# Two-layer graph attention on one core: a fourth query buffer in place of a product buffer, beta added a chunk later, and one pool of five PSUM banks

## The chip, the cores and the metric

The kernel runs on one core of one Trainium2 chip. The core has a matrix engine (TensorE: PE in the profile, with its weight loads as PEld), a vector engine (VectorE: DVE), a scalar engine (ScalarE: ACT), a general engine (GpSimd: POOL) and a synchronising engine (SyncE: SP). POOL issues the indirect DMAs (gathers and scatters) and SP issues most of the plain ones[...]. The metric is the device time of one execution in microseconds, as the median of several runs.

## The reference

The input x has 8 graphs of 2048 nodes with 256 features; one adjacency matrix of 2048 x 2048 holds for all of them, with about 0.4% of its entries set, the diagonal always.

Layer 0 is attention with 4 heads of 64. The scores are clipped to -10..10, masked entries are -10, and the softmax is taken in each chunk of 256 neighbours on its own:

```python
scores = jnp.clip(scores, -10.0, 10.0)
scores = jnp.where(mask == 0, jnp.asarray(-10.0, scores.dtype), scores)
attn = jax.nn.softmax(scores, axis=-1)           # over c within a chunk j
ctx = jnp.einsum('bhnjc,bhjcd->bhnd', attn, vc)
out = ctx @ Wo.T + bo + x                        # then a layer norm with gamma and beta
x = _layernorm(x + out)
```

Layer 1 is a graph attention: logits s_src + s_dst through a leaky ReLU, a softmax over the neighbours, the weighted sum of x @ W, an ELU, a residual and again a layer norm. Everything is float32.

## The kernel before

**Lists of neighbours.** At the start edge_lists (L45) turns each adjacency row into a list of at most 24 neighbours. Nodes are sorted by the number of their neighbours, so that a tile of 128 nodes shares one length (CAPS, L34: 24, 14, 13, 12, 11, 11, 10, 10, 9, 9, 8, 8, 7, 7, 6, 5). If a node has more neighbours than its tile allows, a dense path follows; with this input it does not run.

**Tables.** Two graphs are one group (G = 2; 4 groups). For a group, tables(g, t) (L344) makes for 128 nodes the keys and values (table kv_d in HBM, through the single buffer kvs) and the queries beside x + beta (table qx_d, through the single buffer qs and from xt). Every other call, chunk_x (L322) first transposes a chunk of 256 nodes on PE (L334). Chunks come in by load_x (L314) into two buffers xt; the same buffer takes beta in place on POOL (L352) and is written to qx_d by SP (L353). Only then may load_x fill it again.

**Attention of layer 0.** For each of 64 steps (group g, tile t), fetch0 (L504) gathers the neighbours' rows of kv_d, one indirect DMA (L469) for each place in the list, into "units" of two places, and then the tile's own row of qx_d into one of three buffers qx (L507). Units come from a ring of 14 (L39) that both layers share. scores0 (L511) multiplies keys by queries on DVE (L530); PE sums the products in parts of 8 columns by accumulating transposes (L541) into the bank pr, ACT copies this (L547), and a product with a 0/1 matrix (L551) leaves the scores in PSUM. A third of the units is instead multiplied in place and reduced by DVE alone (L555, L557). A product is laid over the keys of the unit before it; the first one has no such unit and goes into a buffer of its own, prod. softmax0 (L566) clips the scores (L571) and makes the weights; context0 (L588) weights the values (L481 on DVE, L487 on ACT) and PE sums them by accumulating transposes (L494). A step later finish0 (L607) makes the output and both norms; it reads x + beta from the second half of qx (L619, L625), which sets that buffer free. Another step later rows1 (L631) makes the rows of layer 1 (wh_d). In group 1 the lists for layer 1 are made from gathered rows on the way (ACT L459, DVE L460).

**Layer 1** works on two groups at once with the same tiles: fetch1, softmax1, context1, finish1 (L706).

**Order of the work.** The loop from L779 goes through 96 steps. Groups 0 and 1 are layer 0 alone, groups 2 and 3 alternate with the first half of layer 1, and the second half of layer 1 ends the program; while groups 0 to 2 run, the tables of the group after are made in the same steps. Within a group the tiles go from short lists (5) to the longest (24, the ninth step) and back to short ones (L740). In each step the gathers of the step after come first in the source:

```python
        if not tables_first:
            fetch(k + 1)
        scatters()
        if layer == 0:
            scores0(g, t)
            ...
            if g + 1 < NG:
                if i % 2 == 0 and i + NT + 2 < NG * NT:
                    load_x((i + NT + 2) // NT, (i + 2) % NT)
                tables(g + 1, i % NT)
```

The order within each engine's queue is not the source's: a planner lays the instructions of all engines out before the run, by priorities and its own estimate of durations, and adds the waits. The trace shows, for instance, table products of one step between the score transposes of the next. While the lists are made, first_tables (L403) makes the tables of group 0.

**PSUM** [...] Before, they are given out by name: acc two (the sums of both layers), tk two (all of the tables), tf two (scores, and the transposes of rows1), pr one, mf one (finish0, the products of rows1, finish1, and the preparation of the weights).

Of the kernel before, what the change touches and what calls it, by code (L numbers as in the profile page):

```python
# [44 lines left out]
def edge_lists(tc: tile.TileContext, pool, bank, adj, const, ident, rec_d, B, between):  # L45
# [118 lines left out]
    op = bank("mf", 1)[0:1, 0:1]  # L164
# [7 lines left out]
def sparse_path(ctx: ExitStack, tc: tile.TileContext, keep, x, adj, Wq, bq, Wk, bk, Wv, bv, Wo, bo, gamma, beta, W, a,  # L172
# [61 lines left out]
    with tc.tile_pool(name="prep", bufs=2) as prep:  # L234
        for dst, w, scale in ((wq, Wq, 0.125), (wkv[:, :, 0:F], Wk, 1.0), (wkv[:, :, F:], Wv, -1.0 / CH), (wo, Wo, 1.0)):
            wn = prep.tile([P, KC, F], F32, tag="wn", name="wn")
            nc.scalar.dma_start(wn, w.rearrange("(c p) f -> p c f", p=P))
            pt = bank("mf", 1).rearrange("p (c f) -> p c f", c=KC)
# [19 lines left out]
        pt = bank("mf", 1).rearrange("p (c f) -> p c f", c=KC)  # L258
# [4 lines left out]
        pa = bank("mf", 1)[:, 0:KC * 2 * H].rearrange("p (c e) -> p c e", c=KC)  # L263
# [24 lines left out]
        pt = bank("mf", 1)[:, 0:3 * KC].rearrange("p (k c) -> p k c", k=3)  # L288
# [33 lines left out]
    def chunk_x(g, t):  # L322
# [6 lines left out]
        for b in range(G):  # L329
            pt = bank("tk").rearrange("p (c r) -> p c r", r=CH)  # L330
# [12 lines left out]

    def tables(g, t):  # L344
        if t % 2 == 0:
            chunk_x(g, t)
        xT, xC, xt = xTs[g, t - t % 2]
        rows = slice(t % 2 * P, (t % 2 + 1) * P)
        if t % 2:

            xv = xt.rearrange("p k (b f) -> p (k b) f", b=G)
            nc.gpsimd.tensor_tensor(xv, xv, beta_r.unsqueeze(1).to_broadcast([P, 2 * G, F]), op=ALU.add)  # L352
            nc.sync.dma_start(qx_d[g][(t - 1) * P:(t + 1) * P, GF:].rearrange("(k p) f -> p k f", p=P), xt)  # L353
# [4 lines left out]
        for b in range(G):  # L358
            pm = bank("tk")
# [10 lines left out]
        q = bank("tk")  # L370
# [10 lines left out]
        if t == NT - 1:  # L381
# [4 lines left out]
            pv = bank("tk")[:, 0:KC * G].rearrange("p (c b) -> p c b", c=KC)  # L386
# [7 lines left out]
            po = bank("tk")[:, 0:KC * G].rearrange("p (c b) -> p c b", c=KC)  # L394
# [8 lines left out]
    def first_tables(t):  # L403
        if t == 0:
            load_x(0, 0)
        if t % 2 == 0 and t + 2 < NT:
            load_x(0, t + 2)
        tables(0, t)
# [95 lines left out]
    def fetch0(g, t):  # L504
        units = gather(kv_d[g].shape[1], kv_d[g], idx, t)
        qx = work.tile([P, 2 * GF], F32, tag="qx", name="qx", bufs=3)
# [4 lines left out]
    def scores0(g, t):  # L511
# [5 lines left out]
        npe = len(units) - len(units) // 3  # L517
        ps_sc = bank("tf")[:, 0:GH * S].rearrange("p (s e) -> p s e", e=GH)
# [3 lines left out]
        def product(i):  # L522

            u, s0, n = units[i]
            if i:
                room = units[i - 1][0][:, :, 0:GF]
            else:
                room = work.tile([P, UNIT, GF], F32, tag="prod", name="prod", bufs=1)
# [6 lines left out]
        for i in range(0, npe, 4):  # L535
            some = units[i:min(i + 4, npe)]
            pr = bank("pr", 1).rearrange("p (k r) -> p k r", r=P)
# [12 lines left out]
            for k, (u, s0, n) in enumerate(some):  # L550
                nc.tensor.matmul(ps_sc[:, s0:s0 + n, :], prT[0:n * W8, k, :], sel[0:n * W8, 0:n * GH],  # L551
                                 start=(s0 == 0), stop=(k == m - 1 and i + m == npe), skip_group_check=True)
# [226 lines left out]
    for k, (layer, i) in enumerate(seq):  # L779
# [6 lines left out]
        if layer == 0:  # L786
# [13 lines left out]
            if g + 1 < NG:  # L800
                if i % 2 == 0 and i + NT + 2 < NG * NT:
                    load_x((i + NT + 2) // NT, (i + 2) % NT)
# [452 lines left out]
```

## Time and profile before

| What | Value |
|---|---|
| median of 4 runs | 2458.81 us (2455.53 to 2466.82) |
| the profiled execution's own time | 2470.93 us |
| its span, first to last instruction | 2469.2 us |
| granted TensorE clock, mean | 0.882 |
| gathers from kv_d on POOL (L469) | 656, 1262 ns each |
| gathers from wh_d on POOL (L469) | 328, 1243 ns each |
| additions of beta on POOL (L352) | 32, 2478 ns each |
| bytes moved by DMA | 669.10 MB, mean 271 GB/s |
| DMA queue of the gathers, share of 16 engines | 58.4% |
| DMA queue of SP's transfers | 16.9% |

The profile is of one execution, whose own time is 0.5% above the median; shares and durations are read from it, and the medians are what is compared. A row of the groups gives line, engine, operation, the tiles written and read, how often, the busy time and the mean of one in ns, and behind the second bar the time that the engine stood idle just ahead of these instructions, with what ended it. A row of the waits gives who waited for whom: total, number of times, longest. Ends of matmuls are modelled, so a busy PE is not PE at its peak.

### The profile page before, as it was taken

Reading aid. Unit: us, or ns where it says so; the run is one execution under the profiler, and the core shown is the slowest. Engines: PE = TensorE matmul, PEld = TensorE weight load, DVE = VectorE, ACT = ScalarE, POOL = GpSimd, SP = SyncE. Lnnn points to the kernel's source line nnn. Section 1 sums busy time; section 2 is a strip of 40 time slices with the busy share of each in tenths; the row PEclk is TensorE's granted clock in tenths of the full one; section 3 lists DMA queues with packets and bytes.
Section 4 is the critical chain, followed back from the end, with each engine's and each line's share of the span. In section 5 each row is a group of like instructions: output and inputs, shape, how many; then the busy total and the mean of one; then the engine's idle time right before and its main releaser. Section 6 shows DMA issues by size and latency. Waiting matters only on the chain. (4 is left out here: it accounts for less than half of the span.)

```text
span 2469.2 us, 38911 instructions
## 1 busy us (share of the span) xinstructions
PE 1897.9 (77%) x11946; PEld 1622.9 (66%) x11946; DVE 1838.3 (74%) x4071; ACT 1404.6 (57%) x5011; POOL 1512.6 (61%) x1225
## 2 busy tenths in 40 slices
PE   6786787689888889889888988776867775455764
PEld 5675676578667778777777877665756665444653
DVE  5965567778656887767878899887878886556775
ACT  4572453355555556555546766765455677556766
POOL 1122755476544667556677886866768753757884
PEclk8998997799989899999999989887978897687887
DMA  6744977398967869888778998986679974986873
GB/s 227 271 161 156 347 266 257 132 325 300 320 237 263 285 198 355 292 301 302 258 255 298 363 344 281 340 291 244 227 243 343 353 282 172 376 288 228 281 269 109
DMA packets 240749, 669.10 MB, mean 271 GB/s; under 512 B 44455, under 2 KB 70826, under 8 KB 238486
## 3 DMA queue, kind: packets, MB, share of 16 engines
q0 software_dynamic: 156800, 505.01, 58.4%
q1 hardware_dynamic: 80016, 151.56, 16.9%
q10 hardware_dynamic: 3718, 9.97, 1.2%
q8 instruction: 98, 1.61, 0.3%
q14 instruction: 117, 0.96, 0.1%
HBM read 612.79 MB, written 126.36 MB: 299 GB/s over the span
## 5 line engine op out<-in xcount | busy, mean ns | idle before, releaser
L469 POOL DMA_INDIRECT u<-kv_d,idx x656 | 828.1, 1262 | 310.2 <-issue 127.8
L494 PE MATMUL acc<-ident,u 128*128 128x128 f32 x5248 | 729.3, 294 | 186.3 <-DVE u L481 107.3
L494 PEld LDWEIGHTS acc<-ident,u 128*128 128x128 f32 x5248 | 647.7, 153 | 255.7 <-DVE u L481 172.6
L469 POOL DMA_INDIRECT u<-wh_d,idx x328 | 407.6, 1243 | 152.4 <-issue 67.8
L481 DVE TENSOR_TENSOR u<-u,al 128x1024 f32<-128x1024 f32 x280 | 336.5, 1235 | 1.2
L481 DVE TENSOR_TENSOR u<-u,z 128x1024 f32<-128x1024 f32 x266 | 314.9, 1214 | 0.8
L487 ACT ACTIVATE u<-u,z 128x64 f32<-128x64 f32 x1008 | 259.2, 337 | 34.7 <-DVE z L678 34.7
L541 PE MATMUL pr<-ident,u 128*128 128x128 f32 x1472 | 209.4, 292 | 58.3 <-DVE u L530 54.3
L530 DVE TENSOR_TENSOR u<-u,qx 128x1024 f32<-128x1024 f32 x184 | 228.5, 1242 | 26.6 <-DMA u<-kv_d,idx 23.9
L541 PEld LDWEIGHTS pr<-ident,u 128*128 128x128 f32 x1472 | 179.4, 151 | 79.4 <-DVE u L530 71.7
L487 ACT ACTIVATE u<-u,al 128x64 f32<-128x64 f32 x800 | 206.8, 340 | 39.5 <-DVE al L585 36.7
L352 POOL TENSOR_TENSOR xt<-xt,beta_r 128x1024 f32<-128x1024 f32 x32 | 79.3, 2478 | 220.9 <-PE tk L334 179.6
L641 PE MATMUL mf<-wa,x1T 128*128 128x264 f32 x512 | 165.5, 450 | 33.8 <-ACT whs L644 17.6
L507 POOL DMA_INDIRECT qx<-qx_d,node x64 | 77.6, 1212 | 155.9 <-DVE o L625 94.1
L374 PE MATMUL tk<-wq,xT 128*128 128x256 f32 x512 | 146.0, 402 | 28.8 <-ACT kvs L368 28.8
L361 PE MATMUL tk<-wkv,xT 128*128 128x256 f32 x512 | 151.4, 411 | 15.7 <-ACT xC L339 15.5
L613 PE MATMUL mf<-wo,cT 128*128 128x256 f32 x512 | 141.8, 400 | 7.3 <-ACT whs L644 5.2
L641 PEld LDWEIGHTS mf<-wa,x1T 128*128 128x128 f32 x512 | 99.0, 215 | 71.8 <-ACT whs L644 34.0
L365 PE MATMUL tk<-wkv,xC 128*128 128x256 f32 x512 | 144.3, 397 | 0.0
L435 ACT ACTIVATE sq<-o,nm 128x256 bf16<-128x256 f32 x256 | 129.5, 506 | 5.0
L431 ACT ACTIVATE nm<-sums 128x2 f32<-128x2 f32 (+1 forms) x160 | 32.3, 202 | 168.2 <-DVE o L625 90.7
L374 PEld LDWEIGHTS tk<-wq,xT 128*128 128x128 f32 x512 | 93.7, 201 | 42.3 <-ACT kvs L368 33.0
(168 smaller groups left out, 3397.1 us busy)
## 6 DMA issues: line engine op xcount, KB each, us to landing
kv_d<-kvs SPq DMA_DIRECT2D x48, 512.0 KB, 6.3
wh_d<-whs SPq DMA_DIRECT2D x64, 260.0 KB, 5.2
xt<-in_x_dram SPq DMA_DIRECT2D x64, 256.0 KB, 4.7
qx_d<-xt SPq DMA_DIRECT2D x32, 512.0 KB, 3.8
qx_d<-qs SPq DMA_DIRECT2D x64, 256.0 KB, 6.1
x_d<-o SPq DMA_DIRECT2D x64, 256.0 KB, 5.3
xr<-x_d SPq DMA_DIRECT2D x32, 512.0 KB, 4.2
u<-kv_d,idx POOLq DMA_INDIRECT x656, 6.6
```

The costliest lines, as they stand in the source:

```text
L361: nc.tensor.matmul(pm[:, 0:F], xT[:, b * KC + kc, rows], wkv[:, kc, 0:F], start=(kc == 0), stop=False, skip_group_check=True)
L365: nc.tensor.matmul(pm[:, F:], xC[:, b * KC + kc, rows], wkv[:, kc, F:], start=False, stop=(kc == KC - 1), skip_group_check=True)
L374: nc.tensor.matmul(qb, xT[:, b * KC + kc, rows], wq[:, kc, :], start=(b == 0 and kc == 0), stop=False, skip_group_check=True)
L435: nc.scalar.activation(sq, src[:, k, :], AF.Square, bias=nm[:, k:k + 1], accum_out=m2[:, k:k + 1])
L469: nc.gpsimd.indirect_dma_start(out=u[:, k, 0:width], out_offset=None, in_=table, in_offset=bass.IndirectOffsetOnAxis(ap=idx[:, t, s0 + k:s ...
L481: nc.vector.tensor_tensor(pv, pv, av, op=ALU.mult)
L487: nc.scalar.activation(pe, pe, AF.Copy, scale=al[:, e, s0 + k:s0 + k + 1])
L494: nc.tensor.matmul(acc[:, c, :], part[:, k, c * P:(c + 1) * P], ident, is_transpose=True, start=first and k == 0 and c == 0, stop=last and ...
L530: nc.vector.tensor_tensor(prod.rearrange("p k j (s w) -> p k j s w", w=W8), u[:, :, 0:GF].rearrange("p s (k j w) -> p k j s w", k=UNIT, w=W8),
L541: nc.tensor.matmul(pr[0:n * W8, k, :], prod[:, j // (NJ // UNIT), j % (NJ // UNIT), :], ident, is_transpose=True, start=(j == 0), stop=(j ...
L613: nc.tensor.matmul(po[:, b, :], cT[:, b * KC + kc, :], wo[:, kc, :], start=(b == 0 and kc == 0), stop=False, skip_group_check=True)
L641: nc.tensor.matmul(pw[:, 0:F + 2 * H], xT[:, b * KC + kc, :], wa[:, kc, :], start=(kc == 0), stop=(kc == KC - 1))
```

## The change

Four things change together.

- **Queries.** qx has four buffers in place of three; the buffer prod, of the same size, is gone. For that, scores0 multiplies unit 0 in place and reduces it on DVE first, and the PE units are 1 to npe - 1, each product over the unit before it. npe grows by one, so that PE has as many units as before and one fewer is reduced at the end. softmax0 clips three ranges in place of two (two where no unit is reduced at the end).
- **Beta.** The addition and the write to qx_d become add_beta, called two tiles (one chunk) later, at the start of the even call of tables, with the load of the chunk after next right behind it; the last chunk of a table is still treated in the odd call that ends it. load_x is now called from tables alone.
- **PSUM.** tk, tf, pr and mf become one name, m, with five banks that are taken by turns, and sc with one for the scores. acc keeps its two and also serves the check of the lists' lengths once.
- Where the diff below leaves hunks out, they only put `bank("m", 5)` in the place of `bank("tk")` or `bank("mf", 1)`, or `bank("acc")` in one place.

```diff
...
@@ -341,22 +341,30 @@
         xTs[g, t] = xT, xC, xt
         return xT
 
+    def add_beta(g, t):
+
+        xt = xTs.pop((g, t))[2]
+        xv = xt.rearrange("p k (b f) -> p (k b) f", b=G)
+        nc.gpsimd.tensor_tensor(xv, xv, beta_r.unsqueeze(1).to_broadcast([P, 2 * G, F]), op=ALU.add)
+        nc.sync.dma_start(qx_d[g][t * P:(t + 2) * P, GF:].rearrange("(k p) f -> p k f", p=P), xt)
+
     def tables(g, t):
         if t % 2 == 0:
+            if t:
+                add_beta(g, t - 2)
+            if g * NT + t + 2 < NG * NT:
+                load_x(*divmod(g * NT + t + 2, NT))
             chunk_x(g, t)
         xT, xC, xt = xTs[g, t - t % 2]
         rows = slice(t % 2 * P, (t % 2 + 1) * P)
-        if t % 2:
-
-            xv = xt.rearrange("p k (b f) -> p (k b) f", b=G)
-            nc.gpsimd.tensor_tensor(xv, xv, beta_r.unsqueeze(1).to_broadcast([P, 2 * G, F]), op=ALU.add)
-            nc.sync.dma_start(qx_d[g][(t - 1) * P:(t + 1) * P, GF:].rearrange("(k p) f -> p k f", p=P), xt)
+        if t == NT - 1:
+            add_beta(g, t - 1)
         kvs = work.tile([P, 2 * GF + 1], F32, tag="kvs", name="kvs", bufs=1)
         if g == PG:
             nc.scalar.copy(kvs[:, 2 * GF:], rank[:, t:t + 1])
         vk = kvs[:, 0:GF].rearrange("p (j b f) -> p b j f", b=G, j=NJ)
         for b in range(G):
-            pm = bank("tk")
+            pm = bank("m", 5)
             for kc in range(KC):
                 nc.tensor.matmul(pm[:, 0:F], xT[:, b * KC + kc, rows], wkv[:, kc, 0:F], start=(kc == 0), stop=False,
                                  skip_group_check=True)
...
@@ -403,8 +411,6 @@
     def first_tables(t):
         if t == 0:
             load_x(0, 0)
-        if t % 2 == 0 and t + 2 < NT:
-            load_x(0, t + 2)
         tables(0, t)
 
     with tc.tile_pool(name="lists", bufs=1) as pool:
@@ -503,7 +509,7 @@
 
     def fetch0(g, t):
         units = gather(kv_d[g].shape[1], kv_d[g], idx, t)
-        qx = work.tile([P, 2 * GF], F32, tag="qx", name="qx", bufs=3)
+        qx = work.tile([P, 2 * GF], F32, tag="qx", name="qx", bufs=4)
         nc.gpsimd.indirect_dma_start(out=qx, out_offset=None, in_=qx_d[g],
                                      in_offset=bass.IndirectOffsetOnAxis(ap=node[:, t:t + 1], axis=0))
         got0[g, t] = qx, units
@@ -514,27 +520,32 @@
         q = qx[:, 0:GF]
         sc = small.tile([P, GH, S], F32, tag="sc", name="sc")
 
-        npe = len(units) - len(units) // 3
-        ps_sc = bank("tf")[:, 0:GH * S].rearrange("p (s e) -> p s e", e=GH)
+        npe = 1 + len(units) - len(units) // 3
+        ps_sc = bank("sc", 1)[:, 0:GH * S].rearrange("p (s e) -> p s e", e=GH)
         W8 = GH * DP
         qv = q.rearrange("p (k j w) -> p k j w", k=UNIT, w=W8).unsqueeze(3)
 
         def product(i):
 
             u, s0, n = units[i]
-            if i:
-                room = units[i - 1][0][:, :, 0:GF]
-            else:
-                room = work.tile([P, UNIT, GF], F32, tag="prod", name="prod", bufs=1)
+            room = units[i - 1][0][:, :, 0:GF]
             prod = room.rearrange("p k (j w) -> p k j w", w=UNIT * W8)[:, :, :, 0:n * W8]
             nc.vector.tensor_tensor(prod.rearrange("p k j (s w) -> p k j s w", w=W8),
                                     u[:, :, 0:GF].rearrange("p s (k j w) -> p k j s w", k=UNIT, w=W8),
                                     qv.to_broadcast([P, UNIT, NJ // UNIT, n, W8]), op=ALU.mult)
             return prod
 
-        for i in range(0, npe, 4):
+        def reduced(u, s0, n):
+            prod = u[:, :, 0:GF].rearrange("p s (j w) -> p s j w", w=W8)
+            nc.vector.tensor_tensor(prod, prod, q.rearrange("p (j w) -> p j w", w=W8).unsqueeze(1)
+                                    .to_broadcast([P, n, NJ, W8]), op=ALU.mult)
+            nc.vector.tensor_reduce(sc[:, :, s0:s0 + n].rearrange("p e s -> p s e"),
+                                    prod.rearrange("p s j (e d) -> p s e j d", d=DP),
+                                    axis=AX.XY, op=ALU.add)
+        reduced(*units[0])
+        for i in range(1, npe, 4):
             some = units[i:min(i + 4, npe)]
-            pr = bank("pr", 1).rearrange("p (k r) -> p k r", r=P)
+            pr = bank("m", 5).rearrange("p (k r) -> p k r", r=P)
             for k, (u, s0, n) in enumerate(some):
                 prod = product(i + k)
                 for j in range(NJ):
@@ -549,14 +560,9 @@
                 nc.scalar.copy(prT[0:W8, full, :], pr[0:W8, full, :])
             for k, (u, s0, n) in enumerate(some):
                 nc.tensor.matmul(ps_sc[:, s0:s0 + n, :], prT[0:n * W8, k, :], sel[0:n * W8, 0:n * GH],
-                                 start=(s0 == 0), stop=(k == m - 1 and i + m == npe), skip_group_check=True)
-        for u, s0, n in units[npe:]:
-            prod = u[:, :, 0:GF].rearrange("p s (j w) -> p s j w", w=W8)
-            nc.vector.tensor_tensor(prod, prod, q.rearrange("p (j w) -> p j w", w=W8).unsqueeze(1)
-                                    .to_broadcast([P, n, NJ, W8]), op=ALU.mult)
-            nc.vector.tensor_reduce(sc[:, :, s0:s0 + n].rearrange("p e s -> p s e"),
-                                    prod.rearrange("p s j (e d) -> p s e j d", d=DP),
-                                    axis=AX.XY, op=ALU.add)
+                                 start=(s0 == UNIT), stop=(k == m - 1 and i + m == npe), skip_group_check=True)
+        for unit in units[npe:]:
+            reduced(*unit)
         st0[g, t] = ps_sc, sc, min(S, UNIT * npe)
 
 
@@ -567,8 +573,10 @@
         S = CAPS[t]
         n = GH * S
         ps_sc, sc, sp = st0.pop((g, t))
-        for some, dots in ((sc[:, :, 0:sp], ps_sc[:, 0:sp, :].rearrange("p s e -> p e s")), (sc[:, :, sp:], sc[:, :, sp:])):
-            nc.vector.tensor_scalar(some, dots, -10.0, 10.0, op0=ALU.max, op1=ALU.min)
+        nc.vector.tensor_scalar(sc[:, :, UNIT:sp], ps_sc[:, UNIT:sp, :].rearrange("p s e -> p e s"), -10.0, 10.0, op0=ALU.max,
+                                op1=ALU.min)
+        for some in [sc[:, :, 0:UNIT]] + ([sc[:, :, sp:]] if sp < S else []):
+            nc.vector.tensor_scalar(some, some, -10.0, 10.0, op0=ALU.max, op1=ALU.min)
         e = ebuf[:, 0:n]
         ev = e.rearrange("p (e s) -> p e s", s=S)
         nc.scalar.activation(ev, sc, AF.Exp)
@@ -607,7 +615,7 @@
     def finish0(g, t):
         cT = st0.pop((g, t))
         xb = got0.pop((g, t))[0][:, GF:].rearrange("p (b f) -> p b f", b=G)
-        po = bank("mf", 1).rearrange("p (b f) -> p b f", b=G)
+        po = bank("m", 5).rearrange("p (b f) -> p b f", b=G)
         for b in range(G):
             for kc in range(KC):
                 nc.tensor.matmul(po[:, b, :], cT[:, b * KC + kc, :], wo[:, kc, :], start=(b == 0 and kc == 0),
@@ -631,12 +639,12 @@
     def rows1(g, t):
 
         o = st0.pop((g, t))
-        pt = transposed(o.rearrange("p b f -> p (b f)"), "tf", 2)
+        pt = transposed(o.rearrange("p b f -> p (b f)"), "m", 5)
         xT = work.tile([P, G * KC, P], F32, tag="x1T", name="x1T", bufs=1)
         nc.scalar.copy(xT, pt)
         wh = work.tile([P, WW], F32, tag="whs", name="whs")
         for b in range(G):
-            pw = bank("mf", 1)
+            pw = bank("m", 5)
             for kc in range(KC):
                 nc.tensor.matmul(pw[:, 0:F + 2 * H], xT[:, b * KC + kc, :], wa[:, kc, :], start=(kc == 0), stop=(kc == KC - 1))
             nc.scalar.copy(wh[:, b * F:(b + 1) * F], pw[:, 0:F])
@@ -707,7 +715,7 @@
         hTs, xr = st1.pop((p, t))
         sums = small.tile([P, 2 * G], F32, tag="sums1", name="sums1")
         for k, hT in enumerate(hTs):
-            ph = bank("mf", 1)
+            ph = bank("m", 5)
             for c in range(G * KC):
                 nc.tensor.transpose(ph[:, c * P:(c + 1) * P], hT[:, c, :], ident)
 
@@ -773,7 +781,6 @@
             (fetch1 if layer else fetch0)(*at(i))
             fetched[0] += 1
 
-    load_x(1, 0)
     fetch(0)
     waiting = None
     for k, (layer, i) in enumerate(seq):
@@ -798,8 +805,6 @@
             if i:
                 finish0(*at(i - 1))
             if g + 1 < NG:
-                if i % 2 == 0 and i + NT + 2 < NG * NT:
-                    load_x((i + NT + 2) // NT, (i + 2) % NT)
                 tables(g + 1, i % NT)
             if tables_first:
                 fetch(k + 1)
```

## The prediction

> **What bounds the kernel now.** I read the page first, for each engine's share.
>
> ```profile
> span 2469.2 us, 38911 instructions
> PE 1897.9 (77%) x11946; PEld 1622.9 (66%) x11946; DVE 1838.3 (74%) x4071; ACT 1404.6 (57%) x5011; POOL 1512.6 (61%) x1225
> ...
> L469 POOL DMA_INDIRECT u<-kv_d,idx x656 | 828.1, 1262 | 310.2 <-issue 127.8
> ...
> L352 POOL TENSOR_TENSOR xt<-xt,beta_r 128x1024 f32<-128x1024 f32 x32 | 79.3, 2478 | 220.9 <-PE tk L334 179.6
> ...
> L507 POOL DMA_INDIRECT qx<-qx_d,node x64 | 77.6, 1212 | 155.9 <-DVE o L625 94.1
> ```
>
> No engine is full. POOL [...] stands still for 179.6 us until PE has transposed the chunk whose beta it is to add, and for 94.1 us until DVE has finished with a qx buffer. Then the busy time by stage (PE, PEld, DVE, ACT, POOL; clock; DMA share, GB/s):
>
> ```profile
> 560.00:1100.00 540.00, 468.78 (x2943) 400.06 (x2942) 394.32 (x815) 293.11 (x1137) 321.98 (x250) 0.94 0.81 285
> ...
> 1520.00:2060.00 540.00, 407.77 (x2690) 352.43 (x2691) 451.36 (x975) 332.29 (x1221) 369.17 (x292) 0.86 0.80 282
> 2060.00:2469.00 409.00, 224.37 (x1504) 194.88 (x1502) 263.64 (x639) 255.99 (x888) 279.67 (x231) 0.78 0.72 256
> ```
>
> PE leads while tables are made (469 of 540), DVE once they are done (451 of 540), nobody in layer 1 alone. So what a freed POOL is worth is read from those who wait for its gathers; the list of waits (total, times, longest) has them:
>
> ```profile
> DVE o L619 <- PE mf L311: 82.6, 34, 8.7
> PE mf L712 <- DVE xr L716: 74.7, 18, 18.0
> ...
> ACT pl L459 <- DMA u<-kv_d,idx: 58.2, 29, 4.9
> ...
> PE pr L541 <- DVE prod L530: 45.6, 18, 13.0
> ...
> DVE prod L530 <- DMA qx<-qx_d,node: 39.1, 11, 9.8
> ...
> DVE u L530 <- DMA u<-kv_d,idx: 23.9, 10, 6.1
> ```
>
> Last, POOL's and DVE's timelines where the attention starts:
>
> ```profile
> 228.69 2.36 POOL L352 TENSOR_TENSOR xt<-xt,beta_r 128x1024 f32<-128x1024 f32 x1 [14.36 <-PE tk L334]
> 248.19 2.35 POOL L352 TENSOR_TENSOR xt<-xt,beta_r 128x1024 f32<-128x1024 f32 x1 [17.14 <-PE tk L334]
> 250.69 1.02 POOL L469 DMA_INDIRECT u<-kv_d,idx  x1
> ```
> ```profile
> 243.69 1.79 DVE L424 MEMSET u<- 128x2080 f32 x1 [0.38 <-issue]
> 257.37 1.22 DVE L530 TENSOR_TENSOR prod<-u,qx 128x1024 f32<-128x1024 f32 x1 [11.89 <-DMA u<-kv_d,idx]
> 264.65 1.22 DVE L530 TENSOR_TENSOR u<-u,qx 128x1024 f32<-128x1024 f32 x1 [6.05 <-DMA u<-kv_d,idx]
> ```
>
> The first gather is behind an addition that waits 17.14 us; DVE, done clearing units at 245.5, waits 11.89 and 6.05 us for it.
>
> [...] nothing passes the waiting addition. [...] at 461.9 us one L530 took 5.54 us instead of 1.22, beside two additions on POOL (461.75 to 466.4). The change keeps all 32, so I charge nothing for it.
>
> **The change part by part.** Sums are against the profiled execution (2470.9 us; span 2469.2 and 1.7 around it). That is 12 us over the median of 2458.8, 0.5%; I carry the difference over unchanged.
>
> *Beta a chunk later.* An addition then needs a transpose of two steps ago and no longer blocks, save the last of each table (4 of 32), which stays with its own chunk. Moved with it are the qx_d write (SP, 3.8 us to land) and, behind it, two loads of x (4.7 us), which reuse that buffer. The loads keep their step but start 2.4 (addition) + 3.8 + about 0.8 (two issues) = 7 us later. A step takes about 23 us and the load is needed two steps on, so it is hidden; were the addition stuck behind a full fetch, a step's worth of slack would still be left. Without cover it would be 7 us on each of some 28 pairs. What SP has behind the write (kv_d, qx_d, wh_d, x_d) waits as now (SP waits 131.4 us for POOL's additions, 51.2 for the landing), probably less. At the start: with the last two waits gone, gathers can begin at about 231 us instead of 250.7, so both of DVE's waits (18) may go, bounded by the clearing until 245.5. Bounds 0 and -18; I take -15.
>
> *Fourth qx buffer.* It removes POOL's 94.1 us on L625 and most of the rest of the 155.9. Gathers also need one of 14 ring units (POOL waits 174.9 us for PE's L494), so the heavy steps (24 neighbours, 12 units) gain nothing. The consumers' waits: qx 39.1, less 9.8 and 7.5 at two such heavy steps = 21.8; keys 23.9 less 6.1 at the start = 17.8; keys in L555 11.3; together 50.9 on DVE. ACT's 58.2 on L459 holds up PE's next inputs and comes back as part of DVE's 82.6 on L619. Bounds 0 and -109; PE is 87% busy in that stage, so I take under half of DVE's (-22) and a seventh of ACT's (-8): -30.
>
> *No product buffer, unit 0 reduced.* The rows:
>
> ```profile
> L555 DVE TENSOR_TENSOR u<-u,qx 128x1024 f32<-128x1024 f32 x64 | 77.8, 1217 | 10.7 <-DMA u<-kv_d,idx 10.7
> L557 DVE TENSOR_REDUCE sc<-u 128x16 f32<-128x1024 f32 x64 | 77.3, 1211 | 0.2
> ```
>
> The number of products and of reduced units stays. Where the neighbour count is odd and only one unit is reduced (5, 7, 7, 9, 9: five tiles of 16, 20 steps), a full unit is reduced in place of the half one: 1.217 + 1.211 + 0.685 against 0.685 + 0.679 + 1.242, +0.51 us x 20 = +10 on DVE, half of it exposed: +5. Six tiles (24 steps) get a third clamp of 0.17 us: 4 on DVE; with some partial prT copies on ACT (0.27 us, under ACT's slack), +3. And PE's first product comes 1.217 + 1.211 = 2.43 us later after DVE turns to a step. DVE's last product ends as late as before, because today's reductions already lie between the products (707.3 to 713.2 us: product, L555, product, L557, product). So usually PE only shifts its idle time: +8, bounds 0 and 64 x 2.43 = 155.
>
> *Five banks by turns.* acc keeps two; the scores' bank was in effect alone in tf already. Gone are PE's waits for ACT to empty the one mf bank (L641 17.6, L613 5.2) and the second transposed output of layer 1 waiting for the first (L712's 63.8 us in the last stage, less 18.0, 16.6 and 4.4, which are late loads of xr: 25). In that stage DVE still has about 17 us of work in a 20 us step. Bounds 0 and -48; I take -11 and -4: -15. A bank by turns can also be held by finish0's output until DVE reads it; five deep, I charge nothing.
>
> Sum: -15 - 30 + 16 - 15 = -44. 2470.9 - 44 = 2426.9 for a profiled execution, **2415 us** for the median.
>
> **Rivals.** *R1, hidden anyway:* POOL runs ahead sooner but stops at the ring, and PE's 87% and DVE's 84% set the pace. For it: 174.9 us of ring waits, and PE waits of only 8.8 us on L481 from 560 to 1100. Against it: the 50.9 us on DVE and the idle start. Only start, banks and costs are left, and if the banks give little: -15 - 4 + 16 = -3, 2456 us.
>
> *R2, the first product becomes the wait (slower):* in scores0 PE stands behind DVE's multiplication and reduction of unit 0. Price 2.43 us a step. It outweighs gains of 60 less the 8 of small costs once more than 52 / 2.43 = 21 steps expose it fully. PE waited for a first product 18 times today, and 25 by weight loads; the reductions no longer at the end also leave less cover for DVE's 71.1 us wait for the scores. With half the gain (30) and 25 steps: +61 + 8 - 30 = +39, 2498 us; with two thirds (40), +29, 2488.
>
> *R3, all comes off:* the gathers set the pace of light steps too: -18 - 80 + 8 - 25 = -115, 2344 us.
>
> **How the numbers follow.** Forecast 0.50, R1 0.16, R2 0.25, R3 0.09. About 0.5% is what a measurement here can tell from no change (the runs shown lie within 0.46%): 2446.5 to 2471. Forecast and R3 give faster 0.59 (nearly all), R1 same, R2 slower. The likeliest case's own range is 2375 to 2446. For 8 in 10 I take 2345 to 2492: it leaves out about half of R2's upper spread (0.11) and half of R3 with the tail of the forecast (0.06). The low end is R3; the high end lies between R2's two sums.
>
> **What would show it.** Right: POOL's wait of L352 on L334 falls from 179.6 to some 30 us and L507's on L625 from 94.1 to under 30; the first gather starts before 235 us and DVE's first product before 250; no PE wait of mf kind on ACT's whs; DVE's waits for qx halve. Wrong if PE's wait for the first product grows from 45.6 us by more than 50, if POOL's ring wait grows by as much as the others fall (R1), or if the chunk loads appear as PE waits at L334 (8.9 us now). What could undo all of it: the order of instructions on each queue is planned anew, and what it puts behind what cannot be read from the old trace.

## The result, and the profile after

The changed kernel took 2,472.5 us (median of 42 runs, 2,458.1 to 2,486.9), the kernel before beside it 2,465.2 us (63 runs). The ratio is 1.003, 95% interval 1.0017 to 1.0043: a trifle slower, and less than the 0.5% that the prediction had named as the least to be told from no change, where 2,415 us and a gain had been forecast. The profiled execution of the changed kernel took 2,467.6 us, 1.9 of them around the span. The two profiled spans thus differ by -3.5 us (2469.2 and 2465.7) and the medians by +7.2: what follows says where time went and came from, and is not exact to 10 us in its sum.

The page of the changed kernel: the span, each engine's busy time, and the rows of the gathers and of beta's additions.

```profile
span 2465.7 us, 38791 instructions
PE 1860.5 (75%) x11946; PEld 1643.8 (67%) x11946; DVE 1857.9 (75%) x4095; ACT 1392.1 (56%) x5031; POOL 1450.8 (59%) x1225
...
L475 POOL DMA_INDIRECT u<-kv_d,idx x656 | 787.4, 1200 | 443.5 <-PE acc L500 191.3
...
L348 POOL TENSOR_TENSOR xt<-xt,beta_r 128x1024 f32<-128x1024 f32 x32 | 82.8, 2588 | 195.8 <-PE m L334 133.7
```

POOL's gathers have become a little shorter (828.1 to 787.4 us) and its standing still before them longer: 310.2 before, 443.5 now. The list of waits (total, times, longest) says for what. For a unit of the ring,

```profile
POOL u L469 <- PE acc L494: 174.9, 105, 14.1
```

before, and after:

```profile
POOL u L475 <- PE acc L500: 263.6, 109, 18.4
...
POOL xt L348 <- PE m L334: 133.7, 8, 20.3
DVE sc L576 <- PE sc L562: 116.4, 48, 5.9
...
PE m L552 <- DVE u L533: 87.6, 35, 39.1
...
POOL qx L513 <- DVE o L633: 37.2, 5, 9.5
...
POOL u L475 <- DMA kv_d<-kvs: 31.0, 2, 22.5
...
POOL u L475 <- DMA qx_d<-qs: 26.9, 1, 26.9
```

The wait for a query buffer fell from 94.1 to 37.2 us as forecast, the wait for a ring unit rose from 174.9 to 263.6, and two kinds are new: gathers that wait for a table to be written, three times, 58 us together. Busy time by stage (PE, PEld, DVE, ACT, POOL; clock; DMA share, GB/s):

```profile
560.00:1100.00 540.00, 471.55 (x2957) 411.43 (x2956) 388.39 (x816) 295.38 (x1156) 286.20 (x238) 0.91 0.76 273
1520.00:2060.00 540.00, 393.17 (x2660) 350.22 (x2658) 452.22 (x995) 326.89 (x1215) 368.21 (x296) 0.87 0.80 283
2060.00:2465.70 405.70, 232.32 (x1534) 213.54 (x1532) 266.25 (x637) 255.91 (x891) 274.42 (x231) 0.74 0.72 258
```

From 560 to 1,100 us POOL does 35.8 us less than before and the DMA share is 0.76 instead of 0.81, while PE is about as busy as it was (468.8 and 471.6 us). The two later stretches are nearly as before.

**Where the time went and came from.** A step ends when ACT has copied its context (cT, L604 before, L612 after; in layer 1 the second hT). Cut at these ends, the spans of the two kernels, and of the runs that will matter, are as follows (us; "first steps" are the three with which groups 1, 2 and 3 begin; the last 21 to 25 us of each span lie behind the table):

| kernel | first step's end | rest of groups 0 and 1 | first steps | rest of group 2 | rest of group 3 and layer 1's first pass | layer 1 alone |
|---|---|---|---|---|---|---|
| before | 277.7 | 778.4 | 63.5 | 411.0 | 545.8 | 369.1 |
| after | 267.3 | 747.5 | 96.0 | 413.3 | 548.9 | 371.1 |
| five banks alone | 267.0 | 753.2 | 90.6 | 433.1 | 547.5 | 370.9 |
| five banks, lead of 6 | 268.1 | 757.6 | 55.4 | 417.2 | 534.2 | 369.4 |
| all parts, lead of 6 | 276.1 | 751.0 | 62.4 | 401.7 | 540.2 | 373.5 |
| queries alone | 292.9 | 722.0 | 64.0 | 408.0 | 543.3 | 369.3 |
| beta later alone | 283.1 | 776.3 | 66.0 | 432.2 | 550.2 | 365.8 |

The first two rows are the answer to "where": 10.4 us were gained at the start and 30.9 in the steps of groups 0 and 1, together 41. That this is close to the 44 of the forecast is chance: its three terms measured otherwise, as shown below. 32.5 were lost in the three steps with which a group begins, and some 7 later on. POOL's timeline at the first of these changes shows the loss. After:

```profile
610.88 2.87 POOL L348 TENSOR_TENSOR xt<-xt,beta_r 128x1024 f32<-128x1024 f32 x1 [24.73 <-issue]
640.65 1.01 POOL L475 DMA_INDIRECT u<-kv_d,idx  x1 [26.90 <-DMA qx_d<-qs]
```

and before:

```profile
613.99 2.52 POOL L352 TENSOR_TENSOR xt<-xt,beta_r 128x1024 f32<-128x1024 f32 x1
616.67 1.88 POOL L469 DMA_INDIRECT u<-kv_d,idx  x1 [0.15 <-issue]
```

Both gathers are the 165th, the first of group 1. Before, it starts at 616.7 us, 55.8 before group 0's last context is copied (672.5). After, POOL stands still twice. It has 24.7 us to wait for its last addition, since PE transposes that chunk only now (L334, until 610.7 us on PE's timeline; POOL's line names no releaser). Then it waits 26.9 us until group 1's last table has been written. The gather starts at 640.65, about 1 us before the group's end at 641.8; PE then waits 15.4 us for its rows (L552).

The table is late because it is no longer made ahead. Taken from ACT's last copy of a table step (qs, L378 before, L386 after), the table of group g + 1 was finished 85 to 225 us ahead of the context of the same step in group 0 of the kernel before, 59 to 98 in group 1, 43 to 74 in group 2. In the kernel after it is 2 to 21 us in all three. This distance is called the lead below. The order of ACT's queue says the same: so many table steps more than attention steps have been queued when a context is copied (groups 0, 1, 2; 16 steps each):

```
before  7 7 6 6 6 6 5 4 4 4 3 4 3 3 3 3   3 3 3 3 3 2 2 2 2 2 2 2 2 2 2 2   2 2 2 2 1 1 1 1 2 2 2 2 2 2 1 0
after   0 0 0 0 0 0 0 0 0 0 0 0 0 0 0 0   0 0 0 0 0 0 0 0 0 0 0 0 0 0 0 0   0 0 0 0 0 0 0 0 0 0 0 0 0 0 0 0
```

Every ratio in this document compares the faster executions of each kernel, those within 1.5% of its quickest, and as the traces of five runs below (beta later and queries alone at their first trial, the kernel after beside its leads of two and of six) are of slower executions, sizes read from those five are rough.

### The profile page after: what moved, and what is told of

Same layout as the page of the kernel before. It is cut to its first block, busy times and chain, and to the rows that moved or that the text cites. A ratio compares the mean times of both kernels' runs of the same rounds, so it can differ in the third digit from the quotient of the medians.

```text
span 2465.7 us, 38791 instructions
## 1 busy us (share of the span) xinstructions
PE 1860.5 (75%) x11946; PEld 1643.8 (67%) x11946; DVE 1857.9 (75%) x4095; ACT 1392.1 (56%) x5031; POOL 1450.8 (59%) x1225
## 5 line engine op out<-in xcount | busy, mean ns | idle before, releaser
L475 POOL DMA_INDIRECT u<-kv_d,idx x656 | 787.4, 1200 | 443.5 <-PE acc L500 191.3
L552 PE MATMUL m<-ident,u 128*128 128x128 f32 (+1 forms) x1984 | 271.2, 294 | 141.5 <-DVE u L533 87.6
L552 PEld LDWEIGHTS m<-ident,u 128*128 128x128 f32 (+1 forms) x1984 | 241.9, 150 | 158.0 <-issue 106.8
L533 DVE TENSOR_TENSOR u<-u,qx 128x1024 f32<-128x1024 f32 (+1 forms) x248 | 297.2, 1198 | 60.3 <-DMA u<-kv_d,idx 59.2
L348 POOL TENSOR_TENSOR xt<-xt,beta_r 128x1024 f32<-128x1024 f32 x32 | 82.8, 2588 | 195.8 <-PE m L334 133.7
L649 PE MATMUL m<-wa,x1T 128*128 128x264 f32 x512 | 156.0, 453 | 13.4 <-ACT x1T L644 13.2
L369 PE MATMUL m<-wkv,xT 128*128 128x256 f32 x512 | 144.4, 401 | 19.9 <-ACT xT L336 18.3
L373 PE MATMUL m<-wkv,xC 128*128 128x256 f32 x512 | 140.7, 395 | 0.1
L621 PE MATMUL m<-wo,cT 128*128 128x256 f32 x512 | 138.0, 394 | 0.0
L540 DVE TENSOR_TENSOR u<-u,qx 128x1024 f32<-128x1024 f32 (+1 forms) x96 | 110.0, 1147 | 36.9 <-DMA qx<-qx_d,node 32.3
L382 PE MATMUL m<-wq,xT 128*128 128x256 f32 x512 | 135.1, 380 | 0.0
L649 PEld LDWEIGHTS m<-wa,x1T 128*128 128x128 f32 x512 | 105.7, 219 | 36.7 <-ACT x1T L644 18.0
```

Of the source, the lines that this page charges most:

```text
L369: nc.tensor.matmul(pm[:, 0:F], xT[:, b * KC + kc, rows], wkv[:, kc, 0:F], start=(kc == 0), stop=False, skip_group_check=True)
L373: nc.tensor.matmul(pm[:, F:], xC[:, b * KC + kc, rows], wkv[:, kc, F:], start=False, stop=(kc == KC - 1), skip_group_check=True)
L382: nc.tensor.matmul(qb, xT[:, b * KC + kc, rows], wq[:, kc, :], start=(b == 0 and kc == 0), stop=False, skip_group_check=True)
L475: nc.gpsimd.indirect_dma_start(out=u[:, k, 0:width], out_offset=None, in_=table, in_offset=bass.IndirectOffsetOnAxis(ap=idx[:, t, s0 + k:s ...
L533: nc.vector.tensor_tensor(prod.rearrange("p k j (s w) -> p k j s w", w=W8), u[:, :, 0:GF].rearrange("p s (k j w) -> p k j s w", k=UNIT, w=W8),
L552: nc.tensor.matmul(pr[0:n * W8, k, :], prod[:, j // (NJ // UNIT), j % (NJ // UNIT), :], ident, is_transpose=True, start=(j == 0), stop=(j ...
```

## The experiments

**T1, the theory:** banks of one set are handed out in the order in which the program asks for them. With two banks of their own, table steps could run ahead of the attention wherever PE had nothing else to do (six of them in 205 to 256 us, while it waited for the first gathers). In one set of five with the attention's uses, a table step keeps its place between them, and the lead is what the program writes: none. **Rivals** are the prediction's R1 (a freed POOL merely waits at the ring instead) and R2 (unit 0's reduction ahead of the first product takes the gain back).

The runs fell on five occasions, on four chips. They are called A, B, C and D here. The kernel before took 2,624 us on A and 2,629 on B, but 2,472 to 2,473 on C (used twice) and 2,469 on D, near the 2,465 of the first comparison, whose chip is not on record. Ratios are against the kernel before on the same occasion, and a point is a hundredth of its time. A difference between ratios of two occasions is an estimate, since the same kernel's ratio can differ from chip to chip, as will be seen.

**Each part alone, and all with the tables' own banks.** These ran on chip A. The second, third and fourth are the diff's parts taken singly; together the three are the kernel after. The first is the kernel after with

```diff
 # in chunk_x and tables, five places:
-        pm = bank("m", 5)
+        pm = bank("tk")
 # everywhere else:
-        bank("m", 5)
+        bank("m", 3)
```

> The kernel after, but the tables of the next group (transposes, key and value product, queries, biasO) have two PSUM banks of their own again; three banks by turns for all other short uses. Theory T1 (banks taken by turns tie each table step to its place between the attention's banks, so that the tables' lead over the attention is lost and each group starts without work for POOL): table steps run ahead again, 60 us or more between a table step and the end of the attention step beside it, no wait of POOL for a table at the group changes, and 30 to 40 us less than the kernel after, 2430 to 2440, below the kernel before. R1 (a freed POOL only stands at the ring instead): within 0.5% of the kernel after. R2 (unit 0's reduction ahead of the first product takes the gain back): within 0.5% of the kernel after too.

> The kernel before with the banks alone changed: five taken by turns by every short use, one for the scores. T1: slower than before by 20 to 40 us, with the tables made in the step that they belong to and POOL waiting for tables at each group change. R1 and R2: 0 to 15 us faster than before, as predicted for this part.

> The kernel before with beta added a chunk later alone (and the loads of x behind it). T1: POOL's 179.6 us of wait for PE's transposes largely gone, tables still ahead, 5 to 15 us faster than before. R1: POOL's ring wait grows by as much as the other falls, within 0.5% of before. R2 says nothing of it.

> The kernel before with four buffers of queries, no product buffer and unit 0 reduced alone; banks and beta as before. T1: 10 to 20 us faster than before. R2: 10 to 40 us slower, with PE's wait for the first product up by more than 50 us from 45.6. R1: within 0.5%.

Measured: own banks 1.014 (1.008 to 1.019), five banks 1.016 (1.006 to 1.025), beta later 1.013 (1.006 to 1.020), queries 1.010 (1.005 to 1.015). Everything was slower, so three of T1's four expectations on time missed; its reading of the group changes held: the first steps of groups 1 to 3 took 43.0, 39.7 and 39.6 us with the five banks, 25.1, 25.1 and 19.3 with the tables' own. Queries alone cost some 26 us, within the 10 to 40 that R2 had named, but not by R2's wait: PE waited 78 us in all ahead of the transposes of products, and 104 to 110 in the traces of the kernel before. What "slower" meant was open without the kernels before and after beside them, so these came next, with the direct test.

**The lead given back by the program.** These ran on chip B. The five banks stay; the program itself makes each table step earlier, by two steps or by six (LEAD):

```diff
+    for j in range(NT, NT + LEAD):
+        tables(*divmod(j, NT))
...
-            if g + 1 < NG:
-                tables(g + 1, i % NT)
+            if i + NT + LEAD < NG * NT:
+                tables(*divmod(i + NT + LEAD, NT))
```

> The kernel after, unchanged, for its time and trace on the same chip as the next runs. All theories: within 0.5% of before where the chip is as in the first comparison; 0 to 1.5% slower if the chip is like that of the runs of single parts.

> The kernel before, unchanged, for its trace on the same chip as the next runs. T1: tables 40 to 200 us ahead of the attention, first steps of groups 1 to 3 no longer than 27 us, against 28 to 43 us in the kernel after.

> The kernel after, but every table step is made two steps earlier: two of group 1's table steps go between the first gathers and the first scores, and step i makes the table step i + 2. T1: the last gathers of a group are no longer followed by a standing POOL, the first steps of groups 1 to 3 fall to 20 to 27 us (10 to 15 us less each), PE fills its 76 us of waiting at the start: 1.2 to 1.8% below the kernel after, 2430 to 2440 where that takes 2472. R1 (the ring and the pace of PE and DVE set the time): within 0.5% of the kernel after. R2: within 0.5%.

> As the last, six steps earlier instead of two. T1: the group changes cost nothing, as with two; the start, however, has six table steps of some 9 us on PE against 76 us of waiting there: within 10 us of the run with two. R1: within 0.5% of the kernel after.

Measured: after 1.042 (1.036 to 1.048), lead of two 1.018 (1.011 to 1.025), lead of six 1.004 (0.999 to 1.008). The first steps before were 28.6, 19.6 and 17.7 us, the first of them a little over the 27 named, and the kernel after was slower than any theory had said (0 to 1.5% for a chip like the first). The three first steps took 66 us together before, 153 after, 59 and 66 with the leads. T1's main line held: the lead alone is worth 2.4 and 3.8 points of the kernel after, on one chip and one occasion, where R1 and R2 expected nothing. Two details of it did not: the gain of two steps is above the 1.2 to 1.8% named, and six steps were to be within 10 us of two and are 1.4 points better. Two steps already bring the three first steps to 59 us, so what the other four add lies elsewhere, and no trace here says where. On this chip the price of a group change was two to three times that of the first comparison; why, the traces don't say. But the lead of six only came back to the time of before, and DVE waited 72.6 us for the scores in group 1 (17.2 in before on that chip). That gave a second theory, **T2**: besides, unit 0's early reduction makes DVE wait for the scores.

**One part left out at a time, with lead.** These ran on chip C. The first is the five banks alone with a lead of six; the next two leave out the queries' part and beta's part.

> The kernel before with the five banks alone, its table steps (and the loads of x for them) made six steps earlier. T1: the first steps of groups 1 to 3 fall from 39 to 43 us with the five banks alone to 15 to 29, as in before, and the banks' own gain in the steps stays: 1 to 2.5% faster than before. If the lead of the tables is not what the banks took away: slower than before by 1% or more, as with the five banks alone. T2 (besides, unit 0's reduction ahead of the first product makes DVE wait for the scores, so that six steps of lead with all parts gave only the time of before): faster by 1 to 2.5%, DVE's wait for the scores in group 1 at most 45 us.

> The kernel after with six steps of lead, three query buffers and the product buffer as in the kernel before (unit 0 not reduced first): five banks and beta later, with lead. T2: faster than before by 1 to 2.5%, like the five banks with lead; DVE's wait for the scores in group 1 at most 45 us, against 73 us with all parts and the same lead. If beta's place makes the loss instead: within 0.5% of before.

> The kernel after with six steps of lead and beta added where the kernel before adds it: five banks, four query buffers, unit 0 reduced first, with lead. T2: within 0.7% of the run with all parts and six steps of lead, DVE's wait for the scores in group 1 above 60 us. If beta's place makes the loss: 1 to 2.5% faster than before.

> The kernel after with six steps of lead, again, beside the three that leave one part out. T1 and T2: within 0.7% of before where the chip is like the last; 0.5 to 1.5% faster than before on a chip where the kernel after takes 1.003 of before.

Measured: five banks with lead 0.983 (0.980 to 0.987); without the queries' part 0.988 (0.986 to 0.990); without beta's part 0.979 (0.977 to 0.981; 2,419.7 us); all parts with lead 0.980 (0.979 to 0.982; 2,424.9 us). The kernel after itself did not run on this occasion; against its 1.003 from the first comparison the lead makes 0.980, more than the 0.5 to 1.5% that T1 had named. The group change of all parts with lead, POOL's timeline:

```profile
590.24 2.36 POOL L348 TENSOR_TENSOR xt<-xt,beta_r 128x1024 f32<-128x1024 f32 x1
592.76 1.00 POOL L475 DMA_INDIRECT u<-kv_d,idx  x1 [0.16 <-DVE ebuf L583]
```

Group 1's first gather starts at 592.8 us, 55.0 ahead of group 0's end (647.8), and waits for nothing. T2 fell on this chip: leaving unit 0's reduction out made the kernel slower (0.988 against 0.980), and DVE's wait for the scores in group 1 is 31.5 us with all parts, 27.8 without beta's, where more than 60 was expected. Chip B, where T2 came from, was not tried again. R1 fell as well, though the sign that the prediction had named for it is there:

```profile
POOL u L475 <- PE acc L500: 275.7, 116, 19.1
```

POOL waits 275.7 us at the ring in this kernel, more than the 263.6 of the kernel after, and the kernel takes 0.980 of before where that takes 1.003. A wait of POOL at the ring shows that POOL is ahead, and does not by itself say whether that was worth anything.

**What the lead rests on, and each part without it.** These ran on chip D.

> The kernel before with the banks alone changed, without lead, again. T1: 2 to 3.5% slower than the same kernel with six steps of lead (which took 0.983 of before), so 1.003 to 1.018 of before, with first steps of groups 1 to 3 above 28 us. If the stalls come from another part: at or below 0.995 of before.

> The kernel after with the tables' own two banks, again. T1 in its first form (the lead alone was lost): at most 0.99 of before, as with six steps of lead. If the banks by turns are a gain of their own where the lead is kept: between 0.99 and 1.01, with first steps of groups 1 to 3 as short as before's.

> The kernel before with four query buffers and unit 0 reduced first alone, again. By the prediction's terms, -30 + 16 us: 0.994 of before. If those buffers pay only where POOL has a place in the ring for what it gathers: within 0.5% of before; R2: above 1.005.

> The kernel before, banks and all parts as they were, its table steps made six steps earlier. T1: before had its lead already (7 steps at the first, 2 to 3 in group 1, 2 in group 2), so within 0.7% of before. If early tables are the whole gain, whatever the banks: at most 0.988 of before.

Measured: five banks alone 1.008 (1.005 to 1.011), own banks 0.999 (0.997 to 1.001), queries alone 0.982 (0.978 to 0.985; 2,426.4 us), the kernel before with a lead of six 1.006 (1.004 to 1.008). The control holds: early tables are no gain for a kernel that already has them. The five banks alone fell where T1 had put them (1.003 to 1.018), though the third of their first steps is 24.5 us and not above 28. They cost 0.8% here and gained 1.7% with lead on chip C, so the lead is worth some 2.4 points to them, and POOL's timeline shows the same standstill without either of the other parts:

```profile
609.48 2.35 POOL L352 TENSOR_TENSOR xt<-xt,beta_r 128x1024 f32<-128x1024 f32 x1 [14.57 <-issue]
639.47 1.01 POOL L469 DMA_INDIRECT u<-kv_d,idx  x1 [27.64 <-DMA kv_d<-kvs]
```

How far ahead of a group's end the next group's first gather starts, and how long the next group's first step then takes, for the three group changes (us):

| kernel | first gather ahead | first step |
|---|---|---|
| before | 55.8, 58.6, 38.1 | 26.0, 19.2, 18.4 |
| after | 1.1, 2.9, 0.4 | 34.2, 33.0, 28.7 |
| five banks alone | 1.5, 3.1, 2.8 | 35.1, 31.0, 24.5 |
| all parts, lead of 6 | 55.0, 57.9, 39.7 | 24.0, 24.1, 14.3 |
| own banks | 56.9, 54.4, 35.5 | 25.2, 25.1, 15.3 |
| queries alone | 48.7, 12.9, 42.8 | 23.0, 23.8, 17.1 |

The last row shows that a wait for a table need not cost: its second first gather stood 36.2 us until a table was written, and still started 12.9 us before the group's end, which was enough.

Queries alone were the surprise: 1.8% faster, outside all that was expected (0.994, within 0.5%, or above 1.005), and 1.0% slower on chip A. Waits of that kernel:

```profile
POOL u L469 <- PE acc L494: 231.5, 109, 17.5
...
PE pr L546 <- DVE u L527: 65.2, 44, 5.9
...
POOL qx L507 <- DVE o L627: 26.8, 8, 8.0
```

POOL's wait for a query buffer fell by 67 us, and PE's for a product is 65.2 us where it was 45.6 + 54.3 = 99.9 before. R2 falls with that, on this chip. The other wait that R2 had named did grow (DVE's for the scores, 71.1 to 104.3 us), but the kernel is the faster one. Whether the fourth buffer or the early reduction of unit 0 brings the gain was not taken apart. The kernel with the tables' own banks has these queries and the lead, and yet gains nothing. That was against T1's first form (at most 0.99), which took the lost lead for the only loss, and left beta or the three banks as the cause.

**Beta.** These ran on chip C again.

> The kernel after with all banks as in the kernel before: four query buffers, unit 0 reduced first, beta a chunk later. If beta's place takes the gain back: 0.993 of before or more. If the three banks by turns do: 0.978 to 0.988, as the query buffers alone. The prediction's term for beta (-15 us) would give 0.976.

> The kernel before with beta added a chunk later alone, again. If beta's place costs time: 1.005 of before or more, by a later start or a later table. If not: within 0.5% of before, since the 179.6 us that POOL waits for PE's transposes lie for the greater part before 205 us, where POOL has no gather to issue. The prediction's term: 0.994.

Measured: queries and beta 0.989 (0.986 to 0.993), beta later alone 1.009 (1.006 to 1.012). The first lies between its two expectations: against the ratios of chip D, beta takes some 0.8 points of the queries' 1.8 back, and three banks by turns with two for the tables another 1.0 (0.989 to 0.999). The traces place the latter in the steps of groups 0 and 1 (731.9 us without, 760.7 with the three banks); why is open. Beta alone, the wait and POOL's timeline at the start:

```profile
POOL xt L348 <- PE tk L334: 183.4, 11, 24.0
...
POOL qx L513 <- DVE o L631: 120.3, 20, 12.0
```
```profile
232.28 2.35 POOL L348 TENSOR_TENSOR xt<-xt,beta_r 128x1024 f32<-128x1024 f32 x1 [14.23 <-PE tk L334]
251.74 2.35 POOL L348 TENSOR_TENSOR xt<-xt,beta_r 128x1024 f32<-128x1024 f32 x1 [17.11 <-PE tk L334]
254.23 1.02 POOL L475 DMA_INDIRECT u<-kv_d,idx  x1
```

The wait is 183.4 us in 11 waits, against 179.6 in 11 before, and the two blocking additions with their 14 and 17 us still stand ahead of the first gather. POOL's queue, printed in order, is the same in both kernels up to there and well beyond: additions 1 + 7, the scatters of the records, one addition, three gathers of queries, three additions, 29 gathers of keys. In these two kernels, then, the planner put the additions at the same places, whichever step of the program asked for them. In the kernel after the additions have left the start because the five banks keep the tables back (there, and with the banks alone, the queue has no addition between the scatters and the gathers). Why beta later costs 0.8 to 0.9% is not settled. Its trace is slower in group 2 (432.2 against 411.0 us). There POOL waits 33.9 us for one of the three query buffers, 11.6 before (120.3 and 94.1 in the whole span), and DVE 25.0 us for queries at L536, 11.9 before. With the four buffers of the queries' part group 2 loses nothing (405.5 and 408.0), and the loss lies in group 3 (557 against 543; queries and beta against queries alone). With five banks and lead it is 0.980 against 0.979 with the queries' part and 0.988 against 0.983 without; the intervals of each pair overlap, those of the second pair barely. The later write of qx_d and the later loads behind it could be at the root of that; no run took them apart.

## Why the prediction failed, by its own steps

**The step that failed** is the last sentence of "Five banks by turns": that a bank held by another use, "five deep", costs nothing. The term was put at -15 us. Measured alone it is +0.8%, 0.0078 x 2,469 = +19 us, and with the lead written into the program -1.7%, 0.0166 x 2,473 = -41 us. By these two (each from its own chip, so an estimate) the banks' own gain was undersized by 26 us, and the price of sharing the set, 60 us, was left out. The traces of the two differ by 60 us as well, 35 of them in the three first steps. I looked at how long a bank is held, and not at the order in which a shared set is granted. The prediction's closing caution, that the order on each queue is planned anew, pointed at the place, but carried no amount. Five banks by turns paid where the lead was kept (0.983 on chip C) and cost time where the rotation tied a producer that was ahead to its consumer's steps (1.008 on chip D).

**Beta a chunk later** was put at -15 us, for a start freed of two waits. The start did come forward, to the first gather and DVE's first product as forecast (limits 235 and 250 us):

```profile
220.95 1.01 POOL L475 DMA_INDIRECT u<-kv_d,idx  x1 [4.28 <-issue]
```
```profile
248.28 1.16 DVE L540 TENSOR_TENSOR u<-u,qx 128x1024 f32<-128x1024 f32 x1
```

but the banks did it: with them alone the first step ends at 267.0 us, with beta alone at 283.1. The step "an addition then needs a transpose of two steps ago and no longer blocks" failed, since the move in the program moved nothing on POOL's queue there: the two additions still wait 14.2 and 17.1 us. That the move might not reach the queue should have been among the rivals. The size was misread too: of the 179.6 us, 118.7 (seven waits) lie before 165 us, where POOL has no gather to issue. In the kernel after all eight that remain, 133.7 us, lie there, where some 30 us in all had been forecast, and with the five banks alone the same eight stand at 133.6. Measured, this part is +0.9% alone, +21 us.

**Four query buffers, unit 0 reduced first** were put at -30 + 16 = -14 us. Alone they measured 0.0184 x 2,469 = -45 on chip D (+26 on chip A); with five banks and lead 0.5 to 0.8 points, -11 to -19. The mechanism held (the wait on the o that still reads the buffer, 94.1 to 26.8 us alone), and the sizes failed: the gain lies in groups 0 and 1 (56 us), where PE at 87% was taken as the pace, and the +8 for a late first product did not show, except at the very start, where the first step ends 15 us later. DVE's busy time rose by 19.6 us in the kernel after; its added rows had been put at 14.

Singly measured the parts thus add to 19 + 21 - 45 = -5 us, against a forecast of -15 - 15 - 14 = -44 and +7 for the kernel after: two of the three terms had the wrong sign, and the third, three times its forecast, made up for both.

**The banks in layer 1 alone** were to bring the smaller share of the banks' 15 us, 4 (the waits for the one mf bank, the other 11). PE's 63.8 us at the second transposed output are gone, as forecast, and the stage took 371.1 us instead of 369.1 (370.9 with the five banks alone): the wait held nothing up that the stage's length shows.

**The rivals.** The time came out in R1's class, no change, but not by R1: its sign is there (the ring wait grew by 88.7 us, the two others fell by 102.8), yet with lead, the same parts take 48 us off, which R1 denies. R2's figure for the wait (a first product's wait up by more than 50 us) did not come: all of PE's waits ahead of these transposes are some 104 us before and 141 after, and 85 of the latter stand once at the start and at the three group changes. R3's -115 was not reached by any kernel; the best took 53 us off. **Of the signs**, the first gather, DVE's first product and the vanished mf waits were right, no load of a chunk holds PE up, and the query wait is nearly right (37.2, under 30 was named). Wrong were POOL's wait for the transposes (133.7 us) and DVE's waits for queries, which did not halve (39.1 to 32.3 us at L540). The measured time lies in the stated range, but the gain did not come.

**What beats both kernels:** five banks, four query buffers and six steps of lead, 0.979 of before; with beta later as well, 0.980; the queries' part alone, 0.982. They can hardly be told apart. All this holds for chips C and D: on A queries alone took 1.010, on B all parts with six steps 1.004, and the first was tried on neither.

## What to carry to other kernels

Ask of a buffer set that is to be shared not only how many are free but who was running ahead on its own: here sharing made the producer keep the program's order, and its lead had then to be written into the program. A wait counts only where the engine has something to do behind it, so place each wait in time before summing it, and don't take a move in the program for a move on a queue that a planner lays out. Try parts alone, and on more than one chip: on chips C and D two of three parts cost time and the third was worth more than the whole, on A all three cost time.

## What was not expected of the hardware

One and the same pair of kernels stood at 1.003 in the first comparison and at 1.042 on chip B, where the kernel before took 2,629 us instead of 2,465; in the first the three group changes cost 33 us more than before, in the second some 87 us. That seems to go with the chip: C, used on two occasions, gave 2,473 and 2,472 us for the kernel before. The engines' busy times are nearly the same (DVE 1834.7 us on chip B and 1838.3 in the first comparison, POOL 1487.8 and 1512.6, PE 1942.7 and 1897.9), so the added time is mostly waiting; what makes it longer is not known. A gain that was measured on one chip should be measured on another before it is believed.
